# Windowed attention and a Fourier layer on one core: the division right behind the exponential, columns behind the row transforms, transforms back one row later

## The chip, the cores and the metric

The kernel runs on one core of a Trainium2 chip. The metric is the device time of one execution in microseconds: 3679.66 us, the median of three runs (3678.72 to 3681.93). The profile is of one more execution (3666.72 us, of which the trace spans 3664.9 us).

The core has five engines with queues of their own: TensorE (PE; its weight loads are listed as PEld), VectorE (DVE), ScalarE (ACT), GpSimd (POOL) and SyncE (SP), which here issues the transfers. Each engine runs its instructions in the order of the program; semaphores order the engines among each other. In this kernel the order on the four computing engines is the order in which the Python code emits the instructions. So a line that moves in the code moves in its engine's queue.

## The reference, cut to what matters

The input is 32 images of 56 x 56 x 128 in float32. Two layers follow each other, each with a residual and a group norm in front.

```python
# layer 0: shifted 7x7-window attention, 4 heads of 32
x = x + attention(_gn(x))
    # qkv = win @ w_qkv.T; attn = q*scale @ k.T + bias + mask
    # attn = softmax(attn); out = (attn @ v) @ w_proj.T + b_proj
# layer 1: Fourier layer and feed-forward
x = x + feedforward(fourier(_gn(x)))
    # along the width, and along the height:
    #   dct, keep 32 modes, mix channels with w0 (w1) by mode, idct; the sum of both
    # feedforward: relu(h @ W1 + b1) @ W2 + b2   (128 -> 512 -> 128)
```

## The kernel before

One cycle handles one window row (8 windows, 392 tokens) of the attention and, for earlier images, one step of layer 1. There are 8 rows to an image, so 256 rows in all. Layer 1 of an image takes the steps c = 0 to 14; step 0 comes 11 cycles after the image's first row. A cycle therefore holds step c of one image and step c+8 of the image before it.

```python
FF_GROUPS = (HB, HB, HB, HB, HB, 320, 256)     # HB = 512: tokens of a feed-forward group
FF_AT = (7, 8, 9, 10, 12, 13, 14)              # the step of each group
CONV_BEGIN = NWR + 3                           # 11
```

The softmax of row r is four calls, on three buffers `a_sb` used in turn:

```python
def attn_max(r):       # VectorE: max of a;           GpSimd: a - max     (lines 446, 447)
def attn_exp(r):       # ScalarE: exp(a)                                  (line 453)
def attn_divide(r):    # VectorE: sum, reciprocal;    GpSimd: a * 1/sum   (lines 458, 460, 461)
def attn_transpose(im, i, r):  # TensorE: 2 x 4 transposes (472); ScalarE and VectorE copy (480, 482)
```

Layer 1 is made of these:

```python
def transform(im, width, g):   # DCT of 14 lines: matmuls (640), ScalarE copies to y (648)
    # width: reads im.x;  height: reads the columns im.cols[g]
def load_columns(im, g):       # transfer: htok <- scr, 2 x 196 KB
def mix(im, width, g):         # matmuls with w0/w1 (674), copy to z (682), transfer zscr <- z
def load_modes(im, width, g):  # transfer: zT <- zscr (two buffers)
def modes_back(im, width, g):  # inverse DCT of 16 lines (g=3: 8): matmuls (713) into two PSUM banks
    # height: ScalarE copies to xf (729);  width: VectorE adds to xf (724)
def ff_in(im, g):              # res <- scr; GpSimd adds b2 (746); matmuls and relu (758)
def ff_out(im, g):             # matmuls; VectorE adds the residual (782); transfer out <- res
```

There are four PSUM banks for the attention (`pa`) and four for layer 1 (`pc`). At step 0 a norm is computed: `fourier_stats` adds up the parts (`tot`, line 579, VectorE), multiplies with `gmean` on TensorE, and goes on with six small operations on VectorE and GpSimd. The next image's first norm is computed at step 4; it gives `nb` (line 357, VectorE), which a TensorE matmul reads.

The order within a cycle (cuts are marked):

```python
def back_groups(c):
    if c in (4, 5, 6, 7):
        return [(c >= 6, c % 2 * 2 + j) for j in range(2)]   # (width?, g)
    return []

def halves_first(cycle, norm):
    ...                                  # sums of the row of cycle-4 (559, 567, 568)
    attn_qk(im, i, False)                # q, k: matmuls; 377, 386, 394
    ...
    for im, c in fourier(cycle):
        if c == 0:
            im.stats = fourier_stats(im)
            im.cols = {}
            next(im.stats)               # tot
            load_columns(im, 0)
            load_columns(im, 1)
    for im, c in fourier(cycle):
        if c in FF_AT:
            ff_in(im, FF_AT.index(c))
    ...                                  # c == 0: next(im.stats), the norm's matmul and the rest
    if row(cycle - 1)[0]:
        attn_divide(cycle - 1)

# then, in the main loop:
#   eighths:  attn_values(row of cycle-3)            (497, 528, 530)
#   quarters: attn_scores(row of cycle) (428, 436); modes_back of this step's groups
#   attn_max in odd cycles
#   full: in even cycles transpose row cycle-2, attn_max, transpose row cycle-1;
#         the next image's transposes in (273, 285-295, 304) at c = 2 and 3

def halves_last(cycle, norm):
    attn_v(im, i, cycle)                 # 406, 413
    if has_ff(cycle):
        half_columns(cycle)              # c=0: 4 width transforms; 1, 2: 2 height transforms
    half_columns(cycle, True)            # c=3: 4 height mixes; 4, 5: 2 width mixes each
    load_back(cycle + 1)                 # load_modes for the next cycle's modes_back
    next_begin(cycle)                    # c = 0 and 1: load of an image, 784 and 672 KB
    next(norm)                           # at c=4: nb
    im, j = row(cycle - 3)
    if im:
        last_out(cycle)                  # ff_out
        attn_project(im, j)              # matmuls; VectorE adds (545); scr <- xl
    if row(cycle)[0]:
        attn_exp(cycle)
    next(norm)                           # at c=4: the matmul with nb
```

Steps 3 and 11 have no feed-forward. The transposes fall on odd steps.

Of the kernel before, what the change touches and what calls it, by code (L numbers as in the profile page):

```python
# [39 lines left out]
SQRT_S = float(np.sqrt(float(S)))  # L40
QS = HD ** (-0.5)
FF_GROUPS = (HB, HB, HB, HB, HB, 320, 256)
FF_AT = (7, 8, 9, 10, 12, 13, 14)
PW = JP + WT
CONV_BEGIN = NWR + 3

# [2 lines left out]
def swin_fourier_kernel(  # L49
# [348 lines left out]
    def attn_v(im, i, r):  # L398

        pv = attn_bank()  # L400


        for w in (0, 2, 1, 3, 4, 6, 5, 7):
            hs = HALVES[w // 2 % 2]
            j = w // 4 * 2 + w % 2
            nc.tensor.matmul(  # L406
                pv[hs, j * C : (j + 1) * C],
                lhsT=im.xw[i][:, w * WT : w * WT + JP],
                rhs=im.w[:, 2 * C : 3 * C],
                start=True,  # L410
                stop=True,
            )
        nc.scalar.copy(v_sb[r % 3].rearrange("j p c -> j (p c)"), pv)  # L413
# [37 lines left out]
    def attn_exp(r):  # L451
        a3 = a_sb[r % 3].rearrange("p t w j -> p (t w) j")[:, :, 0:WT]
        nc.scalar.activation(a3, a3, AF.Exp)  # L453

    def attn_divide(r):
        a3 = a_sb[r % 3].rearrange("p t w j -> p (t w) j")[:, :, 0:WT]
        sm = small.tile([P, 2 * NWR], F32, tag="sm", name="sm")
        nc.vector.tensor_reduce(sm, a3, axis=AX.X, op=ALU.add)  # L458
        rs = small.tile([P, 2 * NWR], F32, tag="rs", name="rs")
        nc.vector.reciprocal(rs, sm)  # L460
        nc.gpsimd.tensor_tensor(  # L461
            a3, a3, rs.unsqueeze(2).to_broadcast([P, 2 * NWR, WT]), ALU.mult
        )
# [193 lines left out]
    def load_columns(im, g):  # L657

        t = work.tile([TC, CH, C], F32, tag="htok", name="htok", bufs=2)
        src = im.scr.rearrange("h (n r) c -> r h n c", r=2)  # L660
        for r in range(2):
            nc.sync.dma_start(t[r * S : (r + 1) * S], src[r, :, CH * g : CH * (g + 1)])
        im.cols[g] = t
# [28 lines left out]
    def load_modes(im, width, g):  # L692
        l0, n = LINES[g]
        zT = work.tile([P, 4, C], F32, tag="zT", name="zT", bufs=2)
        nc.sync.dma_start(
            zT[:, : n // 4],
            im.zscr[width][l0 : l0 + n].rearrange("(m r) u k c -> (r u k) m c", r=4),
        )
        im.zT[width, g] = zT
# [116 lines left out]
    def row(r):  # L816
        return (images[r // NWR], r % NWR) if 0 <= r < NB * NWR else (None, 0)

    def fourier(cycle):

        b, c = divmod(cycle - CONV_BEGIN, NWR)
        return [(images[b - k], c + k * NWR) for k in (1, 0) if 0 <= b - k < NB]

    def back_groups(c):

        if c in (4, 5, 6, 7):
            return [(c >= 6, c % 2 * 2 + j) for j in range(2)]
        return []

    def load_back(cycle):  # L830
        for im, c in fourier(cycle):
            for width, g in back_groups(c):
                load_modes(im, width, g)

    def halves_first(cycle, norm):
        last, j = row(cycle - 4)
        if last:
            sums = attn_sums(last, j)
            next(sums)
        im, i = row(cycle)  # L840
        if im:
            attn_qk(im, i, False)
        next(norm)
        if last:
            next(sums)
        for im, c in fourier(cycle):
            if c == 0:
                im.stats = fourier_stats(im)
                im.cols = {}
                next(im.stats)  # L850
                load_columns(im, 0)
                load_columns(im, 1)
        for im, c in fourier(cycle):
            if c in FF_AT:
                ff_in(im, FF_AT.index(c))
        for im, c in fourier(cycle):
            if c == 0:
                next(im.stats)
        if row(cycle - 1)[0]:
            attn_divide(cycle - 1)  # L860

    def has_ff(cycle):
        return any(c in FF_AT for _, c in fourier(cycle))

    def half_columns(cycle, rest=False):
        for im, c in fourier(cycle):
            if rest and c != 3:
                continue
            if c == 0:
                for g in range(4):  # L870
                    transform(im, True, g)
            elif c in (1, 2):
                for g in (2 * c - 2, 2 * c - 1):
                    transform(im, False, g)
                    if c == 1:
                        load_columns(im, g + 2)
            elif c == 3:
                for g in range(2):
                    mix(im, False, g + 2 * rest)
            elif c in (4, 5):  # L880
                for g in (2 * c - 8, 2 * c - 7):
                    mix(im, True, g)
# [30 lines left out]
    def last_out(cycle):  # L913
        for im, c in fourier(cycle):
            if c in FF_AT:
                ff_out(im, FF_AT.index(c))

    def halves_last(cycle, norm):
        im, i = row(cycle)
        if im:  # L920
            attn_v(im, i, cycle)
        if has_ff(cycle):
            half_columns(cycle)
        half_columns(cycle, True)
        load_back(cycle + 1)
        next_begin(cycle)
        next(norm)
        im, j = row(cycle - 3)
        if im:
            last_out(cycle)  # L930
            attn_project(im, j)
        if row(cycle)[0]:
            attn_exp(cycle)
        next(norm)

    def next_begin(cycle):
        b, i = divmod(cycle, NWR)
        if b + 1 < NB and i == 3:
            images[b + 1] = image_begin(b + 1)
        if b + 1 < NB and i == 4 and images[b + 1].half:  # L940
            load_part(images[b + 1].x, b + 1, 1)
# [3 lines left out]
    def first_rows(cycle, norm):  # L945
        im, i = row(cycle)
        if im:
            attn_qk(im, i, True)
        if cycle:
            attn_exp(cycle - 1)  # L950
        im3, i3 = row(cycle - 3)
        if im3:
            attn_values(im3, i3, cycle - 3)
        im2, i2 = row(cycle - 2)
        if im2:
            attn_transpose(im2, i2, cycle - 2)
        if cycle:
            attn_divide(cycle - 1)
        if im:
            attn_scores(im, i, cycle)  # L960
            attn_max(cycle)
        if im3:
            attn_project(im3, i3)
        next(norm)
        last, j = row(cycle - 4)
        if last:
            for _ in attn_sums(last, j):
                pass
        if im:
            attn_v(im, i, cycle)  # L970
        if cycle < NWR // 2:
            image_bias(im, 2 * cycle)
        next(norm)
        next_begin(cycle)
        next_groups(cycle)
        if cycle == CONV_BEGIN - 1:
            attn_exp(cycle)
            last, j = row(cycle - 1)
            attn_transpose(last, j, cycle - 1)
        next(norm)  # L980

    def nothing():
        while True:
            yield

    ET = mybir.EngineType
    with tc.manual_schedule(engines={ET.PE, ET.Activation, ET.DVE, ET.Pool}):
        images[0] = image_begin(0)
        for i in range(0, NWR, 2):
            image_groups(images[0], i)  # L990
        for _ in image_norm(images[0]):
            pass
        norm = nothing()
        for cycle in range(NB * NWR + CONV_BEGIN + FF_AT[-1] - NWR + 1):
            if cycle < CONV_BEGIN:
                first_rows(cycle, norm)
            else:
                halves_first(cycle, norm)
                if not row(cycle - 3)[0]:
                    half_columns(cycle)  # L1000
                    half_columns(cycle, True)
                    last_out(cycle)
                    quarters(cycle)
                    load_back(cycle + 1)
                    continue
                if not has_ff(cycle):
                    half_columns(cycle)
                eighths(cycle)
                quarters(cycle)
                if row(cycle)[0] and cycle % 2:  # L1010
                    attn_max(cycle)
                full(cycle)
                halves_last(cycle, norm)
            b, i = divmod(cycle, NWR)
            norm = nothing()
            if i == NWR - 2 and b + 1 < NB:
                norm = image_norm(images[b + 1])
                next(norm)
# [62 lines left out]
```

## Time and profile before

| | |
|---|---|
| time, median of three | 3679.66 us |
| span of the trace | 3664.9 us |
| VectorE's bias add of the scores, L436 | 512 x 558 ns |
| max / sum, L446 / L458 | 256 x 963 ns / 256 x 960 ns |
| subtract / multiply on GpSimd, L447 / L461 | 256 x 1522 ns each |
| exponential, L453 | 256 x 869 ns |
| VectorE's add of the width's inverse transform, L724 (16 lines) | 192 x 615 ns |
| bytes moved | 390.30 MB, mean 106 GB/s |

How to read the views. The page begins with the busy time of each engine, its share of the span and its instructions. TensorE's matmuls are pipelined, so their listed durations overlap; their spacing is the better measure. The list of waits has one line for each pair of a waiting line and what ended the wait: us in total, times, longest. "Issue" is a wait for nothing that the profile shows. A timeline line has the start in us, the length, the engine, the line, what it writes and reads, and how many instructions were merged; in square brackets stands the idle time before it.

### The profile page before, as it was taken

The numbers are of one execution on the slowest core, as the hardware profiler recorded it, in microseconds if no ns is written. First come the engines' busy times: TensorE is split into PE (matmuls) and PEld (weight loads), VectorE is DVE, ScalarE is ACT, GpSimd is POOL, SyncE is SP. The second block draws the span as 40 slices with busy tenths as digits, with TensorE's granted clock in tenths as the row PEclk, the third lists the DMA queues.
The fourth block names the chain that finished last, engine by engine and source line by source line (L and its number), as shares of the span: only waits on it lengthen the run. The fifth ranks groups of instructions, "written<-read, shape, count | busy, mean of one in ns | idle before, by whom it ended". The sixth has DMA issues, their size and how long they took to land.

```text
span 3664.9 us, 161414 instructions
## 1 busy us (share of the span) xinstructions
PE 3567.3 (97%) x72064; PEld 2845.5 (78%) x72064; DVE 2196.4 (60%) x4738; ACT 2138.8 (58%) x4044; POOL 1370.4 (37%) x1421
## 2 busy tenths in 40 slices
PE   7899999999999999999999999999999999999999
PEld 5777778778787778778777877787877778777776
DVE  7756566666665665656666656566566666565641
ACT  5555556655556555666555565555665556655553
POOL 5443343333333433334333434333433343333321
PEclk9999999999999999999999999999999999999999
DMA  4333434344434444343443344443433433343343
GB/s 114 98 101 105 116 91 114 102 111 110 110 92 117 110 108 111 97 111 105 111 110 109 93 113 109 106 116 96 113 105 103 117 100 103 107 110 106 96 111 104
DMA packets 687350, 390.30 MB, mean 106 GB/s; under 512 B 39967, under 2 KB 657600, under 8 KB 686400
## 3 DMA queue, kind: packets, MB, share of 16 engines
q1 hardware_dynamic: 686045, 379.65, 38.2%
q8 instruction: 567, 9.29, 1.1%
q14 instruction: 127, 1.04, 0.1%
q10 hardware_dynamic: 611, 0.32, 0.0%
HBM read 218.29 MB, written 161.48 MB: 104 GB/s over the span
## 4 chain that ended last, share of the span: by engine, by line
PE 89%; DVE 3%; DMA 3%; POOL 2%; ACT 2%; issue 2%; SPq 0%; ACTq 0%; POOLq 0%; DVEq 0%
PE pc L112 36%; PE pa L112 14%; PE pa L406 7%; PE pc L640 6%; PE pa L472 5%; PE pc L713 5%; PE pa L428 5%; PE pc L674 5%; PE pa L497 4%; PE pa L273 3%; DMA zT<-zscr 2%; POOL a L461 1%; DVE sm L458 1%; ACT k L386 1%; DVE k L394 1%
## 5 line engine op out<-in xcount | busy, mean ns | idle before, releaser
L461 POOL TENSOR_TENSOR a<-a,rs 128x784 f32<-128x784 f32 x256 | 389.6, 1522 | 1264.8 <-DVE rs L460 761.4
L112 PE MATMUL pc<-wff,hid 128*64 128x128 f32 x12544 | 742.6, 273 | 3.3 <-issue 1.9
L112 PE MATMUL pc<-xf,wff 128*64 128x512 f32 (+2 forms) x3584 | 719.3, 539 | 0.6 <-DVE xf L724 0.5
L112 PEld LDWEIGHTS pc<-wff,hid 128*64 128x64 f32 x12544 | 704.4, 137 | 10.3 <-issue 4.6
L782 DVE TENSOR_TENSOR res<-pc,res 128x512 f32<-128x512 f32 (+3 forms) x257 | 144.0, 571 | 896.5 <-issue 461.2
L447 POOL TENSOR_TENSOR a<-a,mx 128x784 f32<-128x784 f32 x256 | 389.6, 1522 | 556.6 <-DVE mx L446 511.0
L758 ACT ACTIVATE hid<-pc,b1sb 128x512 f32<-128x512 f32 (+2 forms) x896 | 535.5, 635 | 88.8 <-PE pc L112 86.5
L112 PEld LDWEIGHTS pc<-xf,wff 128*64 128x64 f32 x3584 | 291.7, 137 | 356.0 <-issue 269.9
L377 ACT ACTIVATE q<-pa,bqkv 128x392 f32<-128x392 f32 x256 | 149.7, 585 | 446.6 <-PE pa L112 440.9
L112 PE MATMUL pa<-xw,wn 128*64 128x392 f32 (+1 forms) x2048 | 392.9, 497 | 2.9 <-DVE a L436 2.9
L746 POOL TENSOR_TENSOR res<-res,b2sb 128x512 f32<-128x512 f32 (+2 forms) x256 | 264.3, 1038 | 102.0 <-DMA res<-scr 82.3
L394 DVE TENSOR_SCALAR k<-pa,heads,bqkv 128x392 f32<-128x392 f32 x245 | 167.9, 685 | 222.1 <-ACT k L386 183.6
L453 ACT ACTIVATE a<-a 128x784 f32<-128x784 f32 x256 | 222.4, 869 | 124.1 <-POOL a L447 121.9
L413 ACT COPY v<-pa 128x512 f32<-128x512 f32 x256 | 151.0, 590 | 234.9 <-PE pa L406 234.6
L304 POOL TENSOR_TENSOR xl<-xl,bproj 112x512 f32<-112x512 f32 (+1 forms) x256 | 287.0, 1144 | 0.0
L406 PE MATMUL pa<-wn,xw 128*64 128x128 f32 x4096 | 283.4, 280 | 3.0 <-issue 3.0
L497 PEld LDWEIGHTS pa<-aT,v 49*32 49x32 f32 x16384 | 172.1, 105 | 140.9 <-issue 94.9
L436 DVE TENSOR_TENSOR a<-pa,bm 128x392 f32<-128x392 f32 x512 | 264.1, 558 | 13.6 <-PE pa L428 1.9
L472 PE MATMUL pa<-ident,a 113*113 113x113 f32 x2048 | 249.7, 272 | 15.6 <-POOL a L461 14.5
L480 ACT COPY aT<-pa 113x452 f32<-113x452 f32 x256 | 139.8, 546 | 213.3 <-PE pa L472 213.3
L472 PEld LDWEIGHTS pa<-ident,a 113*113 113x113 f32 x2048 | 218.8, 179 | 40.7 <-POOL a L461 20.9
L112 PE MATMUL pa<-wproj,oT 128*64 128x128 f32 (+1 forms) x3584 | 249.2, 273 | 0.5 <-issue 0.5
(89 smaller groups left out, 5685.1 us busy)
## 6 DMA issues: line engine op xcount, KB each, us to landing
zscr<-z SPq DMA_DIRECT2D x512, 112.0 KB
htok<-scr SPq DMA_DIRECT2D x256, 196.0 KB
zT<-zscr SPq DMA_DIRECT2D x192, 256.0 KB
res<-scr SPq DMA_DIRECT2D x160, 256.0 KB
out_dram<-res SPq DMA_DIRECT2D x160, 256.0 KB
scr<-xl SPq DMA_DIRECT2D x128, 224.0 KB
xl<-in_x_dram SPq DMA_DIRECT2D x32, 784.0 KB
xl<-in_x_dram SPq DMA_DIRECT2D x32, 672.0 KB
```

Source lines behind the costliest of these rows:

```text
L112: nc.tensor.matmul(dst[ps], lhsT=lhsT[:, ps], rhs=rhs, start=start, stop=stop)
L304: nc.gpsimd.tensor_tensor(piece, piece, bproj.unsqueeze(1).to_broadcast([TC, e - a, C]), ALU.add)
L406: nc.tensor.matmul(pv[hs, j * C : (j + 1) * C], lhsT=im.xw[i][:, w * WT : w * WT + JP], rhs=im.w[:, 2 * C : 3 * C], start=True, stop=True,)
L436: nc.vector.tensor_tensor(a[:, 2 * hp : 2 * hp + 2, :, 0:WT].rearrange("p u w j -> p w u j"), ps[hp][:, :RT].rearrange("p (w u j) -> p w u ...
L447: nc.gpsimd.tensor_tensor(a3, a3, mx.unsqueeze(2).to_broadcast([P, 2 * NWR, WT]), ALU.subtract)
L453: nc.scalar.activation(a3, a3, AF.Exp)
L461: nc.gpsimd.tensor_tensor(a3, a3, rs.unsqueeze(2).to_broadcast([P, 2 * NWR, WT]), ALU.mult)
L472: nc.tensor.transpose(pt[:PW, h * P : h * P + PW], a[:PW, h, 2 * hf : 2 * hf + 2].rearrange("p w j -> p (w j)")[:, :PW], ident[:PW, :PW],)
L497: nc.tensor.matmul(po4[u][h * HD : (h + 1) * HD, 2 * f + e], lhsT=v[ks, 2 * f + e, h * HD : (h + 1) * HD], rhs=im.aT[i][f][ks, h, e * JP : ...
L640: nc.tensor.matmul(py[hs, c * 2 * NM : (c + 1) * 2 * NM], lhsT=tok[:, c, hs], rhs=dct_sb, start=True, stop=True,)
L746: nc.gpsimd.tensor_tensor(res[:m, c0:c1], res[:m, c0:c1], b2sb[:m].unsqueeze(1).to_broadcast([m, c1 - c0, C]), ALU.add,)
L758: nc.scalar.activation(hf[:, :n], ph[:, :n], AF.Relu, bias=b1sb[:, f : f + 1])
```

## The change

It does three things, each of which moves calls and adds no work.

The division of a row (`attn_divide`) comes directly behind its exponential, in the same cycle, and both come ahead of the feed-forward's second half and the projection. Before, the division was emitted in the next cycle. It is meant to have the probabilities ready before the transposes ask for them.

The first two columns of step 0 are requested in `load_first`, behind the width transforms and behind the next image's load, instead of at the start of the cycle. It is meant to keep these transfers away from the transforms.

The inverse transforms go from steps 4 to 7 to steps 5 to 8, and each feed-forward group one step later; the last one is now at step 15, and the program runs one cycle more. It is meant to give the modes' way through memory a whole cycle.

```diff
-FF_AT = (7, 8, 9, 10, 12, 13, 14)
+FF_AT = (8, 9, 10, 12, 13, 14, 15)
@@ back_groups
-        if c in (4, 5, 6, 7):
-            return [(c >= 6, c % 2 * 2 + j) for j in range(2)]
+        if c in (5, 6, 7, 8):
+            return [(c >= 7, (c + 1) % 2 * 2 + j) for j in range(2)]
@@ new
+    def load_first(cycle):
+        for im, c in fourier(cycle):
+            if c == 0:
+                load_columns(im, 0)
+                load_columns(im, 1)
@@ halves_first
                 next(im.stats)
-                load_columns(im, 0)
-                load_columns(im, 1)
...
-        if row(cycle - 1)[0]:
-            attn_divide(cycle - 1)
@@ halves_last
         load_back(cycle + 1)
         next_begin(cycle)
+        load_first(cycle)
+        if row(cycle)[0]:
+            attn_exp(cycle)
+            attn_divide(cycle)
         next(norm)
         im, j = row(cycle - 3)
         if im:
             last_out(cycle)
             attn_project(im, j)
-        if row(cycle)[0]:
-            attn_exp(cycle)
         next(norm)
@@ first_rows, in the last cycle before step 0
             attn_exp(cycle)
+            attn_divide(cycle)
@@ the cycles behind the last row
                     half_columns(cycle, True)
+                    load_first(cycle)
                     last_out(cycle)
```

## The prediction

> **What bounds the kernel now.** I read the page's first part, then who waited for whom, then the timeline of single cycles.
>
> ```profile
> span 3664.9 us, 161414 instructions
> PE 3567.3 (97%) x72064; PEld 2845.5 (78%) x72064; DVE 2196.4 (60%) x4738; ACT 2138.8 (58%) x4044; POOL 1370.4 (37%) x1421
> q8 instruction: 567, 9.29, 1.1%
> ```
>
> TensorE is busy for all but 98 us of the span, so nothing done on another engine is worth more than what it takes out of those 98 us. Some 20 to 27 us of them lie in the first 92 us (the first of the 40 slices shows 7 tenths), which the change hardly touches. Its own waits:
>
> ```profile
> PE pc L640 <- issue: 20.5, 20, 1.8
> PE pa L472 <- POOL a L461: 14.5, 32, 0.5
> PE pc L713 <- DMA zT<-zscr: 12.1, 17, 3.1
> PE pa L112 <- DVE nb L357: 9.6, 2, 4.9
> PE pa L112 <- DVE tot L579: 3.9, 1, 3.9
> ```
>
> The columns are the wait in total, how often, and the longest. The first three are one each of the change's three parts. From here on, step c is the c-th cycle of an image in the second layer. A cycle holds step c of one image and step c+8 of the image before; c=0 and c=8 share one.
>
> **Wait 1, the attention's division.** The chain of waits at the start of a step c=3, which has no feed-forward to hide anything:
>
> ```profile
> 1035.31 0.88 DVE sm L458
> 1036.22 0.26 DVE rs L460
> 1036.61 1.53 POOL a L461
> 1038.19 1.05 PE pa L472 x8
> ```
>
> The second half of the transposes stands until GpSimd's division (1.52 us) is done. Start to start, 16 transposes before the image groups take 2.41 us here; elsewhere they take 1.77. So it costs 0.64 us an image.
>
> **Wait 2, "issue" in the row transforms.** At c=0 the columns are requested just ahead of the transforms:
>
> ```profile
> 1102.66 1.79 SPq L662 DMA_DIRECT2D htok<-scr  x4
> 1106.28 1.92 PE L640 MATMUL pc<-dct_w,xl 112*64 112x64 f32 x60
> 1109.21 1.68 PE L640 MATMUL pc<-dct_w,xl 112*64 112x64 f32 x51 [1.01 <-issue]
> ```
>
> TensorE stops in the middle of one line's matmuls, waiting for no engine. There are 144,128 matmuls and weight loads and 567 instruction packets, so about 256 instructions to a packet of 16 KB. Counting the trace's TensorE instructions in order, these stops in L640 all come at the same place modulo 256: at block boundaries. In the stalled cases the block's packet started 1.6 to 2.7 us after the block before it had begun to execute; in blocks just as dense that stall little, 0.8 to 1.0 us. The packet takes about 1.0 to 1.3 us, and another 1.35 us pass until execution. The 4 x 196 KB of columns are in the DMA engines just then.
>
> **Wait 3** is the mode reload zT after its own mixes: the loads for c=4 and for c=6 are issued right behind the mixes that write what they read.
>
> **What the Trainium skill says.** "Runtime: NRT & Kernel Launch", section "Instruction fetch mechanics": an engine's instructions come in 16 KiB blocks of 256 over a DMA queue of its own, the next block while the current one runs; it calls the cost mostly hidden. The count agrees; "hidden" does not hold here, with 20.5 us of TensorE waits. "DMA: Bandwidth & Descriptors", section "Queues, rings and completion order": each DMA engine takes turns between queues packet by packet, which is why columns can delay a fetch; the late starts above fit. "Perfetto Trace Analysis", section "Identifying Performance Opportunities": with one engine saturated, look for the gaps on that engine and the semaphore behind each. That is the method here.
>
> **Part 1: division moved.** Nothing is added: 256 times sum (960 ns), reciprocal (253 ns) on VectorE and multiply (1,522 ns) on GpSimd, each half a cycle earlier. In most cycles VectorE idles about 5 us before the residual add L782, so 1.2 us fit. The 0.64 us at c=3 go: 32 x 0.64 = -21 us. The new order also puts sum and reciprocal ahead of three things: L782, the projection's add L545 and, at c=4, the next image's bias nb. They now wait for max, subtract, exponential, sum.
>
> **Part 2: columns behind the transforms.** Fetches during the transforms should start at about +0.9 us instead of up to +2.7. A 256-instruction block at this density (224 instructions in 3.27 us, so 256 in 3.7) then needs 0.9 + 1.1 + 1.35 = 3.35 us and is hidden. I take -17 of the 20.5 us. The columns have about 14 us until c=1 needs them; 784 KB of them behind 784 KB of the next image at the 238 to 272 GB/s seen in such stretches need about 6 us. Hidden.
>
> **Part 3: transforms back and feed-forward a row later.** The work is the same, in other company. Loads of zT for widths get a whole cycle after their mixes: -15 us (12.1 on the matmuls and, from the same list, 3.3 on the weight loads). Tokens per cycle and step, before and after: the 256-token group moves from c=6 to c=7, and the two full backs of the width move from c=6 to c=7 as well. That cycle also transposes. So the shortest cycle now has the longest VectorE chain. It must be followed in detail, counting from the start of q and k, with durations and spacings from the timeline:
>
> - TensorE: scores end at 4.77 us (as in the 256-token cycle before), backs 1.64, transposes 1.77, v 0.92, second feed-forward matmuls 1.75, projection 0.87, so c=0 begins at 11.72; its q, k and first feed-forward matmuls (1.32 + 3.43) end at 16.47, and there the statistics matmul needs `tot`.
> - VectorE: bias adds from 4.98; the four adds of the backs to 8.06 (the last two must wait for matmuls); a copy of the transposes, then max to 9.56; GpSimd subtract to 11.25; exponential to 12.16; sum and reciprocal to 13.46; L782, L545, L559, k, L568 and `tot` at 0.4, then about 0.7 us each: 17.1.
>
> Before, this point was close already:
>
> ```profile
> 1102.44 0.69 DVE L579 TENSOR_REDUCE tot<-part 112x64 f32<-112x512 f32 x1
> 1103.57 0.29 PE L112 MATMUL pa<-tot,gmean 112*64 112x64 f32 x4
> ```
>
> 0.44 us of slack become a wait of about 0.7 us: 29 images x 0.7 = +20 us. At c=0 itself the statistics hold VectorE for 2.06 us after that matmul, then oT, the score adds and now the backs' adds. The first transform needs a PSUM bank that such an add empties: about 0.45 us late, 29 x 0.45 = +13. At c=4 the same walk starts with L545 at 1.95 us instead of 0.2 (behind the sum of c=3) and gives score adds to 8.5, max 9.5, subtract 11.2, exponential 12.1, sum and reciprocal 13.3, nb 13.45; TensorE, without backs in this cycle now, asks for nb at 13.1: 30 x 0.35 = +10. At the end, the last image has a mix's time more before its first reload: +2.
>
> **The sum.** -21 - 17 - 15 + 20 + 13 + 10 + 2 = -8 us. The gains are measured waits; the losses are my walk through queues, where I chose the later time twice. A wait also gives the instruction fetch time, so losses and remaining fetch stalls overlap. Of the 45 us of losses I therefore take about three quarters, 33: -53 + 33 = -20 us, 3660 us.
>
> **Rivals.**
> - *All three waits go and nothing replaces them.* For it: VectorE and ScalarE are at 60% and 58%, and the 5 us of idle before L782 swallow the division in most cycles. It gives -53 us: 3627. Against it: the one tight cycle above.
> - *A new wait takes the place of the old.* `tot` and nb, both VectorE, at their full size or worse (1.3 us and 0.8 us an image): 29 x 1.3 = +38 and 30 x 0.8 = +24, with the transforms' bank +13. Then -53 + 75 = +22: 3702. For it: in c=7 the chain through max, subtract, exponential, sum is serial over three engines and the cycle is only 11.7 us.
> - *The fetch stalls only move.* c=0 now runs 128 (values) + 64 (scores) + 96 (backs) + 32 (v) + 224 (transforms) = 544 dense instructions at 79 per us, where it ran 448. Boundaries with a whole dense block before them rise from (448-256)/256 = 0.75 to (544-256)/256 = 1.1 an image. If the columns were not what delays fetches, L640 would go from 20.5 to about 37 us. The late packet starts speak against it. It would put the time 33 us above the 3660, near 3693.
>
> **Range and chances.** From 3625 (everything hidden) to 3695 (a rival in full) lies the range; the middle is 3660. A gain of 2% is 74 us and more than all the waits the change could remove, a loss of 2% needs more than a new 1.5 us wait an image on top of the lost gains: 3% each, 94% within 2%.
>
> **What would show it.** Right: among TensorE's waits, L472 on L461 near 0, L713 on zT near 0, L640 on issue under 5 us, and a new line "L112 <- DVE tot" of 10 to 30 us with some 29 cases; the exponential's own timing against the z and y copies unchanged. Step 1 is wrong if L472 still waits at c=3; step 2 if L640's stops remain at block boundaries though no columns are in flight. I am wrong as a whole if `tot` comes before its matmul in the short cycle (then the time is near 3630), or if L545's delay holds ScalarE's square and with it the feed-forward's copies (then TensorE waits for pc banks, and it is above 3695).

## The result, and the profile after

| | before | after |
|---|---|---|
| time, median | 3679.19 us (4 runs) | 3667.68 us (4 runs, 3663.85 to 3669.34) |
| ratio | | 0.9968, 95% interval 0.9951 to 0.9986 |
| span of the trace | 3664.9 us | 3662.0 us |

The changed kernel is faster by 0.3%, some 12 us of the 20 us predicted, and the 3660 us lay 8 us too low. The trace of before is of one of its quickest executions (3666.72 us; of the 73 timed ones in the groups below the quickest took 3670.01), so the spans differ by 2.9 us where the medians differ by 11.5. What follows about single waits is counted inside each trace.

The page of the changed kernel begins with the same picture as before. Its last line here is the chain of waits:

```profile
span 3662.0 us, 161441 instructions
PE 3574.7 (98%) x72064; PEld 2832.1 (77%) x72064; DVE 2216.2 (61%) x4738; ACT 2147.2 (59%) x4044; POOL 1368.1 (37%) x1421
PE 77%; DVE 15%; ACT 3%; POOL 3%; issue 2%; DMA 1%; SPq 0%; POOLq 0%; DVEq 0%; ACTq 0%
```

The same line before:

```profile
PE 89%; DVE 3%; DMA 3%; POOL 2%; ACT 2%; issue 2%; SPq 0%; ACTq 0%; POOLq 0%; DVEq 0%
```

VectorE's busy time is hardly longer (2216 against 2196 us), yet it now stands on the chain for 15% of the span, where it stood for 3%. That points to its order and not to its load. TensorE's waits in the changed kernel (us in total, times, longest):

```profile
PE pa L112 <- DVE nb L357: 18.5, 22, 5.0
PE pa L112 <- DVE tot L579: 18.1, 26, 4.8
PE pc L713 <- issue: 7.9, 9, 1.3
...
PE pc L640 <- issue: 1.6, 3, 1.0
...
PE pa L472 <- POOL a L461: 0.3, 1, 0.3
```

The three waits that the change aimed at are gone: L640 on issue 20.5 to 1.6 us, L472 on the division 14.5 to 0.3, L713 on zT 12.1 to no case at all. In their place stand `tot` and `nb`, both VectorE's, and L713's stops on issue have grown from 4.0 to 7.9 us. One cycle in which `tot` is late, in the timeline of the changed kernel (start, length, and in brackets the idle time before):

```profile
1097.78 0.97 DVE L458 TENSOR_REDUCE sm<-a 128x16 f32<-128x784 f32 x1 [2.08 <-ACT a L453]
...
1099.23 0.68 DVE L545 TENSOR_TENSOR xl<-pa,xl 112x512 f32<-112x512 f32 x1
...
1101.86 0.69 DVE L579 TENSOR_REDUCE tot<-part 112x64 f32<-112x512 f32 x1
1102.69 0.34 PE L112 MATMUL pa<-tot,gmean 112*64 112x64 f32 x4 [0.44 <-DVE tot L579]
```

VectorE stands idle for 2.08 us ahead of L458: the row's sum is next in its queue, and the exponential isn't done. Behind it wait the residual add, the projection's add and everything that leads to `tot`. TensorE pays 0.44 us here.

Where the time went, counted from one `tot` matmul to the next: the 28 images in the steady middle take 112.36 us each before and 111.94 after, which is -11.7 us in all. The stretch from the start to the third of these matmuls is 3.0 us longer and the end 5.8 us. Those two aren't losses of the same kind: a feed-forward group and some inverse matmuls now come behind the matmul that I count from, so work has moved from the start to the end. It makes the start's own loss bigger and the end's smaller. Between the first two of these matmuls, where no older image has a feed-forward to cover anything, TensorE's waits add up to 19.9 us in the changed kernel against 12.3 before, `tot` and `nb` alone 11.8 against 3.9.

### The profile page after: what moved, and what is told of

It reads as the page before. It is cut to its first block, busy times and chain, and to the rows that moved or that the text cites. A ratio compares the mean times of both kernels' runs of the same rounds, so it can differ in the third digit from the quotient of the medians.

```text
span 3662.0 us, 161441 instructions
## 1 busy us (share of the span) xinstructions
PE 3574.7 (98%) x72064; PEld 2832.1 (77%) x72064; DVE 2216.2 (61%) x4738; ACT 2147.2 (59%) x4044; POOL 1368.1 (37%) x1421
## 4 chain that ended last, share of the span: by engine, by line
PE 77%; DVE 15%; ACT 3%; POOL 3%; issue 2%; DMA 1%; SPq 0%; POOLq 0%; DVEq 0%; ACTq 0%
PE pc L112 30%; PE pa L112 12%; PE pc L640 6%; PE pa L406 5%; PE pc L674 5%; PE pa L428 5%; PE pa L472 5%; PE pa L497 4%; PE pc L713 3%; PE pa L273 3%; POOL a L447 2%; DVE sm L458 2%; DVE a L436 2%; DVE xf L724 2%; ACT a L453 2%
## 5 line engine op out<-in xcount | busy, mean ns | idle before, releaser
L458 DVE TENSOR_REDUCE sm<-a 128x16 f32<-128x784 f32 x256 | 248.2, 970 | 693.8 <-ACT a L453 692.9
L758 ACT ACTIVATE hid<-pc,b1sb 128x512 f32<-128x512 f32 (+2 forms) x896 | 526.7, 632 | 76.3 <-PE pc L112 74.2
L528 DVE TENSOR_SCALAR oT<-pa,bqkv 128x98 f32<-128x98 f32 (+2 forms) x768 | 171.1, 278 | 271.1 <-PE pa L497 271.1
L436 DVE TENSOR_TENSOR a<-pa,bm 128x392 f32<-128x392 f32 x512 | 264.9, 560 | 24.1 <-PE pa L428 0.5
L406 PEld LDWEIGHTS pa<-wn,xw 128*64 128x64 f32 x4096 | 220.9, 137 | 37.7 <-issue 8.9
L394 DVE TENSOR_SCALAR k<-pa,heads,bqkv 128x392 f32<-128x392 f32 x245 | 167.2, 683 | 135.7 <-ACT k L386 133.1
L782 DVE TENSOR_TENSOR res<-pc,res 128x512 f32<-128x512 f32 (+3 forms) x257 | 140.2, 556 | 180.3 <-PE pc L112 146.5
```

Source lines behind the costliest of these rows:

```text
L406: nc.tensor.matmul(pv[hs, j * C : (j + 1) * C], lhsT=im.xw[i][:, w * WT : w * WT + JP], rhs=im.w[:, 2 * C : 3 * C], start=True, stop=True,)
L436: nc.vector.tensor_tensor(a[:, 2 * hp : 2 * hp + 2, :, 0:WT].rearrange("p u w j -> p w u j"), ps[hp][:, :RT].rearrange("p (w u j) -> p w u ...
L758: nc.scalar.activation(hf[:, :n], ph[:, :n], AF.Relu, bias=b1sb[:, f : f + 1])
```

## The experiments

All ratios are to the kernel before, from runs on the same chip. The rows come from four groups of runs, in which the kernel before had medians from 3677.67 to 3682.09 us; rows of different groups are compared by their ratios. My theory after the result: the three waits were worth what I had taken for them, each part took its own one away, and part 1's early place in VectorE's queue made the new waits. The rivals: a part alone brings nothing because the next wait takes over, or it was another part that did it.

| run | what differs from before | median us | ratio, 95% interval |
|---|---|---|---|
| changed kernel | all parts | 3667.68 | 0.9968 [0.9951, 0.9986] |
| only_divide | part 1 | 3682.14 | 1.0002 [0.9992, 1.0012] |
| only_columns | part 2 | 3682.22 | 0.9999 [0.9989, 1.0008] |
| only_later | part 3 | 3675.76 | 0.9985 [0.9978, 0.9992] |
| no_columns | parts 1 and 3 | 3669.96 | 0.9965 [0.9953, 0.9977] |
| late_divide | all, division behind the projection | 3659.69 | 0.9936 [0.9920, 0.9952] |
| late_no_later | late division and part 2, no part 3 | 3670.66 | 0.9967 [0.9956, 0.9978] |
| small_first | all, 256-token group first | 3701.48 | 1.0052 [1.0040, 1.0065] |
| columns_act | columns asked for by ScalarE | 3669.09 | 0.9975 [0.9963, 0.9986] |
| late_columns_act | late_divide with columns_act | 3653.05 | 0.9933 [0.9917, 0.9948] |
| late_backs_first | late_divide, backs ahead of scores at step 8 | 3658.47 | 0.9944 [0.9930, 0.9959] |
| late_ff_between | late_divide, step 0's transforms behind `ff_out`, the next image's load behind the projection | 3666.53 | 0.9965 [0.9951, 0.9979] |

### Part 1 alone

```diff
 # halves_first: attn_divide(cycle - 1) removed; halves_last:
         next_begin(cycle)
+        if row(cycle)[0]:
+            attn_exp(cycle)
+            attn_divide(cycle)
         next(norm)
 # ... attn_exp(cycle) behind attn_project removed
```

> The division alone behind its exponential; columns and steps as before. My theory: the wait of the transposes L472 for the division goes (about -20 us in the trace); the nb wait stays out in the long run, because step 4 still holds the backs and TensorE asks later, but at the start, without a feed-forward, nb waits about 5 us. In all near -15 us, 0.996 of before, no wait for tot. Rival (the early division itself is what costs): waits for tot and nb of 10 us or more each appear here too, and the time is that of before within 5 us.

It missed: no gain at all. The rival has the time right, but not for its reason: the waits for `tot` (4.8 us, once) and `nb` (11.9 us, three times) are hardly longer than before (3.9 and 9.6). The wait that part 1 was made for is gone, and another has doubled. Waits of TensorE in this run:

```profile
PE pc L713 <- DMA zT<-zscr: 24.8, 34, 3.3
PE pc L640 <- issue: 21.1, 19, 1.8
```

The division's wait at step 3 is out of the cycle (12.36 us to 11.88, median), and step 4 is longer (14.98 to 15.69). My first reading was that TensorE simply arrives at zT sooner, and that whoever removes one wait finds the next. The timeline around the end of step 3 says something else. Before:

```profile
1044.49 0.69 DVE L545 TENSOR_TENSOR xl<-pa,xl 112x512 f32<-112x512 f32 x1 [2.29 <-PE pa L112]
1045.25 0.32 SPq L551 DMA_DIRECT2D scr<-xl  x1
1046.78 6.72 SPq L695 DMA_DIRECT2D zT<-zscr  x4
```

With part 1 alone:

```profile
1050.24 0.97 DVE L458 TENSOR_REDUCE sm<-a 128x16 f32<-128x784 f32 x1 [2.96 <-ACT a L453]
...
1051.41 0.63 DVE L545 TENSOR_TENSOR xl<-pa,xl 112x512 f32<-112x512 f32 x1
...
1052.11 0.32 SPq L551 DMA_DIRECT2D scr<-xl  x1
1052.65 4.65 SPq L695 DMA_DIRECT2D zT<-zscr  x3
```

VectorE idles 2.96 us for the exponential, and the projection's add comes after the sum: 4.57 us after the start of the cycle's last mixes (1046.84), where it is 2.84 us before (1041.65 to 1044.49). SyncE issues the store of that add's result (L551) before the loads of zT (L695), so the loads stand behind it. From the last mix matmul of step 3 to the first inverse matmul of step 4 it is 7.96 us (median of 27 images) against 7.29 before: zT itself comes 0.67 us later, and step 4 loses 0.71 us where step 3 gained 0.48.

### Late division without part 3

This run tells the two readings apart. The division still comes in the exponential's own cycle, but behind the projection; the exponential keeps the early place that part 1 gave it, and the columns are asked for as in part 2; transforms back and feed-forward stay at their old steps. The call at the start of the next cycle is gone, as in part 1.

```diff
     last_out(cycle)
     attn_project(im, j)
+if row(cycle)[0]:            # attn_exp stays ahead of last_out
+    attn_divide(cycle)
```

> Division behind the projection and the columns of part 2, but the backs and the feed-forward at their old steps (no part 3). Theory A, part 1 needs part 3: the transposes' wait on the division goes, but the same time is spent a cycle later on zT, whose loads start behind the same mixes: ratio 0.998 to 1.001, wait on zT above 20 us in total. Theory B, the early position of the division took the gain of the run with part 1 alone: ratio 0.993 to 0.996 here.

The ratio lies between the two forecasts but nearer the second: 0.9967. The wait on zT stays far under the 20 us of the first. Waits of TensorE:

```profile
PE pc L640 <- issue: 26.4, 19, 2.3
PE pc L713 <- DMA zT<-zscr: 14.3, 18, 3.1
```

zT waits about as it did before (12.1 us, 17 times), L545 stands 2.84 us behind the start of the mixes again, the way from the last mix to the inverse matmul is 7.29 us again, and step 3 keeps its 11.88 us. So in part 1 alone the wait wasn't handed on for want of time: the early place of the division had delayed a store, and the store the loads behind it. My first reading fell. Of the gain some goes into L640's stops, which are 6 us longer than in the trace of before; the run of part 2 alone shows that two kernels with the same order can differ by nearly as much (25.5 against 20.5 us).

### Part 2 alone, and everything but part 2

```diff
-                load_columns(im, 0)          # halves_first, c == 0
-                load_columns(im, 1)
...
         next_begin(cycle)
+        load_first(cycle)
```

> The first columns behind the transforms alone. My theory (the columns' transfers hold up the instruction packets): TensorE's issue wait in L640 falls from 20.5 to under 5 us, -17 us, 0.995 of before. Rival (the density of the instructions makes the stops): the issue wait in L640 stays at 15 us or more and the time does not move.

> The changed kernel without its part 2 (columns asked for at the start of step 0 again; division and row shift as changed). Theory A, part 2 changes the order on no engine, SyncE's included, so it does nothing: ratio to the kernel before as the changed kernel's, 0.995 to 0.998, and TensorE's issue wait in L640 stays below 4 us. Theory B, the moved columns are what took L640's 20 us away: that wait is back at 15 us or more and the time is 10 to 15 us above the changed kernel's.

Part 2 alone makes 0.9999, without it the changed kernel is what it was with it (0.9965 and 0.9968), and its L640 line stays nearly empty. For part 2 alone the rival named the right numbers, but density is not what they show. Waits of TensorE, first with part 2 alone:

```profile
PE pc L640 <- issue: 25.5, 21, 2.0
```

then with parts 1 and 3 without it:

```profile
PE pc L640 <- issue: 1.5, 4, 0.6
```

The reason is in the queue of SyncE, here of the changed kernel at step 0:

```profile
1103.11 2.71 SPq L662 DMA_DIRECT2D htok<-scr  x4
1110.61 1.12 SPq L118 DMA_DIRECT2D xl<-in_x_dram  x2
```

and before, where L662 starts at 1102.66:

```profile
1111.02 1.11 SPq L118 DMA_DIRECT2D xl<-in_x_dram  x2
```

In the code `load_first` comes behind the next image's load; in the queue the columns (L662) are still 7.5 us ahead of it (L118), as they are in the same cycle of the kernel before. Only the four computing engines take the code's order: the kernel asks for it with `tc.manual_schedule(engines={ET.PE, ET.Activation, ET.DVE, ET.Pool})`, where SyncE is missing. In the trace of part 2 alone all 2068 transfers that SyncE issues stand in the order of the kernel before, and so does every instruction of VectorE, ScalarE and GpSimd; of TensorE's 72,064 matmuls 14 are listed in another place. Part 2 does nothing.

### The columns really moved

An engine whose order is the code's can ask for the columns. ScalarE does it here, behind its copies of the transforms:

```diff
-            nc.sync.dma_start(t[r * S : (r + 1) * S], ...)
+            (engine or nc.sync).dma_start(t[r * S : (r + 1) * S], ...)
+                load_columns(im, 0, nc.scalar)   # in load_first
+                load_columns(im, 1, nc.scalar)
```

> The kernel before, with the first two columns issued from ScalarE's queue behind the copies of the row transforms, so that they truly go out behind them (the change leaves their place in SyncE's queue as it was). Theory A (the columns in the DMA engines delay the instruction packets): TensorE's issue wait in L640 falls from 20 to 25 us to under 5 us, and the time by about 15 us, 0.996 of before. Theory B (the density of the instructions, whatever is in flight): the issue wait in L640 stays at 15 us or more and the time within 5 us of before.

0.9975, some 9 us of the 15 forecast, and the wait didn't fall under 5 us. Waits of TensorE in L640:

```profile
PE pc L640 <- issue: 14.2, 7, 7.5
```

The single 7.5 us is in the first image. The other six are in the transforms of step 1; the stops in step 0 are gone, and step 0 falls from 15.69 us to 14.90 in the mean. Step 1, which reads the columns soon after they were requested, grows from 15.20 to 15.75. The instruction packets show why; each brings one block of 256 TensorE instructions. At the block boundaries inside step 0's transforms of the kernel before, the packet of the next block starts 2.09 us after the current block has begun (median of 27), and TensorE stops at 19 of the 27. In columns_act the packet starts after 0.75 us (median of 25), and TensorE stops at none. The instructions are as dense as they were. So columns in the DMA engines do delay the instruction packets, as the prediction had it, and some 70% of what is won by moving them is lost in the next cycle.

### Part 3 alone

```diff
-FF_AT = (7, 8, 9, 10, 12, 13, 14)
+FF_AT = (8, 9, 10, 12, 13, 14, 15)
-        if c in (4, 5, 6, 7):
-            return [(c >= 6, c % 2 * 2 + j) for j in range(2)]
+        if c in (5, 6, 7, 8):
+            return [(c >= 7, (c + 1) % 2 * 2 + j) for j in range(2)]
```

> Backs and feed-forward one step later alone. My theory (tot waits because the division stands ahead of the residual and projection adds): no wait for tot, since the division is still behind tot; the zT wait of 12 us goes; L640 keeps its issue wait and may grow to 30 us, as step 0 now runs 544 dense instructions with the columns in flight; the first transform waits for a bank (7 us); L472 keeps its wait. In all within 10 us of before. Rival (the short cycle with backs and transposes alone makes tot late): a wait for tot of 10 to 20 us in some 25 cases, and the time 10 us or more above before.

0.9985, within the forecast; but the stops in L640 went instead of growing, and the wait for the bank is four times the 7 us. Waits of TensorE:

```profile
PE pc L640 <- DVE xf L724: 26.8, 22, 1.2
PE pa L472 <- POOL a L461: 13.3, 29, 0.5
```

This part empties "L640 on issue" and zT, but in their place the first transform waits 1.2 us for its PSUM bank, which the backs' add L724 frees late: the backs of step 8 stand ahead of the transforms now. While TensorE waits there, the next block of instructions arrives: the packets at these boundaries still start late, 1.84 us (median of 25), yet TensorE stops at only 3 of the 25. `tot` is in time (one late case of 3.9 us, at the start), so part 3's short cycle alone doesn't make it late; part 1's order is needed as well.

### Late division with parts 2 and 3

> The changed kernel, with the division emitted behind the residual and the projection instead of ahead of them, in the same cycle. My theory: tot and nb waits go (18 us each on TensorE in the changed kernel, with the start), L472's wait stays away; about -25 to -30 us against the changed kernel, near 3640, 0.989 to 0.991 of before. Rival (the short cycle itself): tot keeps a wait of 10 us or more, and the time is within 10 us of the changed kernel, 0.994 to 0.997 of before.

The diff to the changed kernel is the one of "late division without part 3", with the early call removed. It is the better kernel, 0.9936 (its interval and the changed kernel's just touch, at 0.9952 and 0.9951), though by less than I had expected. In the short cycle, timeline of this run:

```profile
1092.04 0.87 ACT L453 ACTIVATE a<-a 128x784 f32<-128x784 f32 x1 [1.37 <-POOL a L447]
1092.70 0.69 DVE L545 TENSOR_TENSOR xl<-pa,xl 112x512 f32<-112x512 f32 x1 [0.39 <-PE pa L112]
1093.31 0.96 DVE L458 TENSOR_REDUCE sm<-a 128x16 f32<-128x784 f32 x1
...
1096.32 0.69 DVE L579 TENSOR_REDUCE tot<-part 112x64 f32<-112x512 f32 x1
...
1097.24 0.28 PE L112 MATMUL pa<-tot,gmean 112*64 112x64 f32 x4
```

VectorE does L545 while the exponential runs, and the sum finds its data without a stop (no bracket). `tot` ends at 1097.01, and the matmul doesn't wait for it. Waits of TensorE in this run:

```profile
PE pc L713 <- issue: 13.1, 10, 3.2
PE pa L112 <- DVE nb L357: 10.8, 3, 4.9
PE pc L640 <- issue: 9.8, 13, 1.4
PE pa L406 <- issue: 8.9, 7, 2.1
...
PE pa L112 <- DVE tot L579: 4.8, 1, 4.8
```

`tot` (4.8 us, once) and `nb` (10.8 us, three times) are back at the few cases of the start. In return TensorE stops for instructions in three lines. I counted the trace's TensorE instructions, those of its sequencer included, and added up the distances from start to start of over 0.3 us that lie at every 256th of them, from 200 us on. These are the gaps of the table, each row from a single trace:

| run | gaps at block boundaries, us |
|---|---|
| before | 41.6 |
| only_columns (same order as before) | 50.3 |
| changed kernel | 24.1 |
| no_columns (same order as the changed kernel) | 30.0 |
| only_later | 29.6 |
| late_divide | 46.1 |
| late_no_later | 52.7 |
| columns_act | 26.5 |
| late_columns_act | 27.6 |

The waits that late division takes from the changed kernel, 13.3 us of `tot` (18.1 to 4.8) and 7.7 of `nb` (18.5 to 10.8), are about the 22 us that these gaps grow by; two kernels with the same order differ by 6 to 9 us, so the match to one us is chance. A wait for another engine gives the fetch its time; take the wait away and part of it comes back as "issue". That late division gains in spite of it is shown by the ratio; the two single traces differ by only 4.6 us, so I can't put the rest of that gain to lines.

### The shortest cycle made longer

```diff
-FF_GROUPS = (HB, HB, HB, HB, HB, 320, 256)
+FF_GROUPS = (256, 320, HB, HB, HB, HB, HB)
```

> The changed kernel with the feed-forward groups in the order 256, 320, 5 x 512 tokens, so that the cycle of steps 7 and 15 has a 512-token group, 3.4 us more matmuls than with 256, and the short group is at step 8. Theory A, tot is late because the shortest cycle has the longest VectorE chain: the wait on tot falls from 18 us to under 6 us, and the time by 5 to 12 us (ratio 0.993 to 0.996), less what the now shorter cycle of step 8 and 0 gives back in fetch stalls or bank waits. Theory B, tot is late only because of the order on VectorE (sum and reciprocal ahead of the residual add), whatever the cycle's length: the wait on tot stays at 12 us or more.

1.0052. The first theory missed. The second has its sign, a wait of 12 us or more, but neither foresaw that the wait would more than double and the kernel fall behind the one before. The wait and the timeline of this run, same place:

```profile
PE pa L112 <- DVE tot L579: 45.5, 32, 4.8
...
1112.48 0.69 DVE L394 TENSOR_SCALAR k<-pa,heads,bqkv 128x392 f32<-128x392 f32 x1 [0.47 <-ACT k L386]
1113.79 0.69 DVE L579 TENSOR_REDUCE tot<-part 112x64 f32<-112x512 f32 x1
...
1114.63 0.34 PE L112 MATMUL pa<-tot,gmean 112*64 112x64 f32 x4 [1.25 <-DVE tot L579]
```

I had looked at the length of the cycle. What counts is the stretch from the scores, where VectorE's chain starts, to the `tot` matmul. TensorE needs 12.61 us for it in the changed kernel (scores at 1089.64, ready for `tot` at 1102.25) and 12.64 here (1100.74, 1113.38): the second matmuls of step 15 have grown, but the first matmuls of step 8, ahead of `tot`, have shrunk with the group that moved there, and the longer first matmuls of step 15 lie ahead of the scores. VectorE needs 13.74 us to the end of `tot` against 12.91: L782 takes 0.63 instead of 0.36, and L394 waits 0.47 for ScalarE's k. The 0.83 us more are the wait: 0.44 became 1.25. In all `tot` costs 27 us more than in the changed kernel, of some 33 by which the two traces' steady middles differ; the rest was not followed.

### Three attempts on top of late division

The columns by ScalarE as well (the diff of "the columns really moved" on late_divide):

> late_divide with the same move of the first columns to ScalarE's queue. Theory A: the issue waits of 10 us in L640 and part of those in L713 and L406 at step 0 go, 8 to 15 us less than late_divide, 0.990 to 0.991 of before. Theory B: the same as late_divide within 4 us.

The backs of step 8 ahead of the scores, so that their adds free the bank earlier:

```diff
+        for im, c in backs:
+            for width, g in back_groups(c) if c == 8 else ():
+                modes_back(im, width, g)      # ahead of attn_scores; c != 8 stays behind
```

> late_divide with the backs of step 8 emitted ahead of the scores of that cycle. Theory (the first transform waits for a PSUM bank that VectorE's backs empty late, behind statistics, oT and score adds): the 0.26 us an image at the first L640 go, 7 us less than late_divide. Rival: the transforms then arrive earlier and wait for instructions instead, and the time is that of late_divide within 4 us.

The width transforms of step 0 behind `ff_out`, and with them the load of the next image behind the projection:

```diff
             last_out(cycle)
+            if zero and has_ff(cycle):       # zero: the cycle of step 0
+                half_columns(cycle)
             attn_project(im, j)
+        if zero:
+            next_begin(cycle)                # the next image's load
...
```

> late_divide with the row transforms of step 0 emitted behind the feed-forward's second half. Theory B (density): the dense run of 544 instructions is split by 128 slow ones, so issue waits in L640 fall under 3 us and the bank wait goes, 10 to 20 us less than late_divide. Theory A (columns in flight): the same, since the columns have landed by then. It does not tell A from B; it tells whether fetch and bank together are worth 15 us. Rival: ScalarE's y copies and exponential come late and hold the next cycle; the time is that of late_divide or above.

The first has the lowest time of all, 3653.05 us, but its ratio's interval nearly coincides with that of late_divide (0.9917 to 0.9948, 0.9920 to 0.9952), so it isn't shown to be better, and the 8 to 15 us of the first theory didn't come. Waits of TensorE in it:

```profile
PE pc L640 <- DMA htok<-scr: 10.5, 6, 7.1
PE pc L640 <- issue: 8.0, 8, 1.6
```

Here the columns come late: 7.1 us of the 10.5 are one case, and the gaps at block boundaries fall to 27.6 us. The second run shows the exchange most cleanly. Waits of TensorE in it:

```profile
PE pc L640 <- issue: 16.9, 14, 1.8
```

The wait for the bank is gone, L640's stops are 7.1 us longer than in late_divide, and the time is no better (0.9944), as its rival had it. The third is slower than late_divide (0.9965), with 11.3 us of stops left in L640 and 6.1 us in the feed-forward that now runs ahead of the transforms. So the forecast of 10 to 20 us less missed, and its rival came true in time; whether by ScalarE's copies was not followed.

## Why the prediction was right or wrong

The time, 3667.68 us, lies in the range and the ratio within 2%. The sum's single terms, measured by adding up the distances from one TensorE matmul's start to the next over the 28 steady images, changed kernel less kernel before:

| term | predicted us | measured us |
|---|---|---|
| part 1, the division's wait | -21 | -20.1 |
| part 2, stops in L640 | -17 | -18.5, but not by part 2 |
| part 3, zT | -15 | -8.4 (what is left at L713 are stops at blocks) |
| `tot` | +20 (29 x 0.7) | +15.2 (28 x 0.54) |
| the transforms' bank | +13 (29 x 0.45) | +6.3 (28 x 0.23) |
| nb | +10 (30 x 0.35) | +10.0 (28 x 0.36) |
| transposes in, L273 | none | +7.2 (56 x 0.13) |
| first image | none | about +8 of TensorE's waits |

- **Part 1** was right in its main term and in its losses: the sum ahead of the projection's add delays it, and `tot` and `nb` come late, in the tight cycle that the walk found. The walk is within 0.2 us: counted from q and k, `tot` ends at 16.95 us (17.1 predicted) and TensorE is ready for it at 16.65 (16.47 predicted). late_divide undoes that order alone, and both waits go. Not foreseen: without part 3 the same order also delays a store on SyncE and the zT loads behind it. Nor were the 7.2 us at L273 foreseen: only_divide, late_no_later and late_divide, which have the division in its exponential's cycle, show 7.1 to 7.2 us there, only_later none. So step 3 gains 0.48 us an image and not 0.64. What makes them was not followed.
- **Part 2 is the step that failed**: "Fetches during the transforms should start at about +0.9 us instead of up to +2.7 ... I take -17 of the 20.5 us." The step took for granted that the call's new place in the code moves the transfer. SyncE's order isn't the code's, and the columns went out as before. The mechanism itself holds: columns_act, which does move them, has its packets start at +0.75 us and no stops in step 0. That the sum still got its -17 is luck, for other parts brought it; and for the same reason the sign it had named, L640's stops under 5 us, came true without the step.
- **Part 3** took its wait on zT away. In the rival "the fetch stalls only move" I counted the backs of step 8 as more dense instructions and hence more boundaries. only_later shows the other effect of the same backs: L640's stops shrink by 18.0 us, but the wait for the bank ahead of them grows by 29.0. In the changed kernel the bank takes 6.3 us and `tot` 15.2, and the stops stay away as well; in late_divide, without the wait for `tot`, only 6.1 us of the stops are gone, against 6.4 for the bank. So the -18.5 was paid for with the new waits.
- **The three quarters** that I took of the losses: 33 us of 45. Measured were 15.2 + 6.3 + 10.0 = 31.5, so these were not what made the time longer than predicted. The gains came to 47.0 us in place of 53, and two terms were missing: L273, and the first image, where no feed-forward covers the exponential's chain. The steady terms of the table add up to -8.3 us; the 28 images measured -11.7, and the rest is spread over many small differences. All this is between two single traces with 2.9 us between them, so it orders the terms; it can't account for the 8 us between 3660 and the median.
- **The readings**: the -15 us of part 3 counts one wait twice. The 3.3 us on the weight loads are a single case at 159.4 us, and the 3.1 us of the matmul behind it are among the 12.1. The rival's growth of L640 to 37 us doesn't follow from its own boundaries, 20.5 x 1.125 / 0.75 = 31.
- **The rivals**: "all three waits go and nothing replaces them" (3627) is out, for `tot` and `nb` do. "A new wait takes their place" was right in kind, with 31.5 of its 75 us. "The fetch stalls only move" is out for L640 (1.6 us); some stops did move, to L713.

The Trainium skill's page "Runtime: NRT & Kernel Launch", section "Instruction fetch mechanics", has blocks of 256 instructions, which every run here agrees with, and calls the cost of crossing a boundary mostly hidden. Most crossings are: before, TensorE stops at 45 of 542. But the stops add up to 24 to 53 us a run. "DMA: Bandwidth & Descriptors", section "Queues, rings and completion order", has the engines take turns between rings by packets; columns_act fits that.

**Open**: where late_divide's further gain over the changed kernel lies (of the 4.6 us between the two traces 1.8 lie ahead of the third `tot` matmul and 2.8 in the steady middle, but the ratios differ by some 12 us); why the gaps at boundaries of two kernels with the same order differ by 6 to 9 us; and whether columns asked for between step 0 and step 1 could be hidden on both sides. None of these was tried.

## What to carry to other kernels

An instruction that waits for a long chain belongs behind everything in its queue that is ready sooner: the same division cost the projection's add 1.7 us in one place and nothing three lines further down. Before crediting a moved transfer, read the issuing queue in the new trace, because its order may not be the code's. And on an engine busy for 97% of the span, count a removed wait only after asking what it was giving time to; in the two traces of changed kernel and late division about as much as was removed came back as instruction fetch.

## What the runs showed of the hardware

Waits for other engines and for instructions trade against each other: late_backs_first and late_divide each removed a wait of TensorE and got stops at block boundaries instead, +7.1 us in L640 and +22 us over the whole trace, where runs of the same order differ by 6 to 9. Transfers in flight delay TensorE's instruction packets: with the columns moved out of step 0's transforms they started after 0.75 us instead of 2.09. And a TensorE that waited more was also granted less, once: between the first two `tot` matmuls the granted clock (the share of full speed) was 0.93 before and 0.90 after, where TensorE's waits were 12.3 and 19.9 us; in the next image it was 1.00 in both. That the longer waits lowered the clock was not tried.
